# A fused attention and mixture-of-experts kernel: order of the last expert tiles, blocks of the ending, a sum on VectorE, and the check on the softmax sums

## The chip, the cores and the metric

The kernel runs on one core of a Trainium2 chip. The metric is the device time of one launch in microseconds (us), taken as the median of the runs. Beside it there is one profiled execution, from which every duration below comes.

## The reference

The input is one image `x` of 256 channels and 48 x 48 positions, all in float32. The 2304 positions are called tokens. Two layers follow each other.

```python
# layer 0: group norm, then softmax attention over all 4 x 2304 = 9216 head rows
x = x + conv_attention(group_norm(x), Wq, Wk, Wv, Wo)
# layer 1, on tokens t[2304, 256]: attention through 64 slices, then a mixture of 8 experts
t = t + slice_attention(layer_norm(t), W0, Ws, Wqkv, Wout)
xf = layer_norm(t)
top_w, top_i = top_k(xf @ Wg + bg, 2)            # two experts for each token
w = one_hot(top_i) * softmax(top_w)
for e in range(8):
    t = t + w[:, e] * (gelu(xf @ W1[e] + b1[e]) @ W2[e] + b2[e])   # 256 -> 1024 -> 256
out = t transposed back to channels x positions
```

## The kernel before

**Layer 0.** The queries are walked in `NQB` = 18 blocks of 512. For each block the loop runs over 36 pairs of key tiles. TensorE makes scores `s`, ScalarE makes `p` = exp(`s`), VectorE adds `p` into `acc`, and TensorE multiplies `p` with the values into `av`. No row maximum is subtracted. So the kernel keeps, for each block, the largest partial sum and the smallest sum: `extremes()` writes both into `ends_of`, reading `both` in SBUF and the sums `pb` in PSUM. `invert()` has by then written `rinv` = 1/`pb`. Small pieces of work such as these are popped from a list, one after each pair. Much later `judge()` reduces `ends_of`, compares it with `HIGH` and `LOW`, and leaves a flag `bad`. All engines read this flag at the very end, and a branch on it skips a second, safer computation.

**Routing.** VectorE finds the two best experts of each token: `first_max` writes a 0/1 mask into `sel[:, 0]` and then `sel[:, 1]`, each 128 partitions x 18 token tiles x 8 experts. TensorE counts them over the partitions into `pto` (with a matrix of ones) and `pin` (with a triangle, `not_before`). A scan over `pto` on VectorE gives `upto`, and from there a chain on VectorE, ScalarE (`what`) and TensorE (`pw`) gives the list `slot_t`, which says what token lies in which row of which expert tile. The matmuls into `spin`, issued by `busy(n, bank)`, compute nothing that is used.

**Experts.** There are `SURE` = 36 tiles of 128 rows that are always there, numbered 0 to 35, after a few extra ones. For a tile s, the pieces are:

- `rows` gathers its tokens (GpSimd, an indirect DMA) and `load_w1` its weights (SyncE), two tiles ahead;
- `turn` transposes the rows on TensorE (`pt`), and VectorE copies them to `xT`;
- `first` multiplies with W1 in 32 TensorE instructions into `ph`, and ScalarE makes 8 Gelus into `hid`;
- `second` multiplies with W2 in 16 TensorE instructions into `py`, and VectorE adds the bias and scales with the routing weight into `y`;
- `scatter` adds `y` into the token array `t_d` in HBM (GpSimd, an indirect DMA that reads and writes). One scatter waits for the one before to have landed.

TensorE's order is written out by hand: first(s), then second(s-1) with turn(s+1) inside it. At the end of the loop this gives, in short, F33 S32 F34 S33 S34 F35, and then the ending.

**Ending.** The last tile, 35, is not scattered. SyncE loads `t_d` back in the five blocks of `TBLOCKS`, from the last (256 tokens) to the first (512 each), once scatter 34 has landed. Meanwhile TensorE runs S35. Then, for each block and each half `c` of the channels, `columns` transposes the loaded tokens into a bank of `ph` (three banks in turn), a matmul with `here` (which row of tile 35 belongs to which token) adds the contribution of tile 35, and VectorE (`c` = 0) or ScalarE (`c` = 1) copies the bank to `ob`. The write to the output is issued by SyncE, for the last two blocks by ScalarE. TensorE runs one `columns` ahead of the matmul with `here`.

Nearly all instructions bear line 58 in the profile, since a helper issues them. They are told apart by their tiles.

Of the kernel before, what the change touches and what calls it, by code (L numbers as in the profile page):

```python
# [9 lines left out]
FP = mybir.dt.float32  # L10
AF = mybir.ActivationFunctionType
ALU = mybir.AluOpType
AX = mybir.AxisListType
PSUM = bass.MemoryType.PSUM

P = 128
C = 256
NT = 2304
NTT = NT // P
# [7 lines left out]
LOW, HIGH = 1e-12, 1e20  # L27
# [3 lines left out]
E = 8  # L31
# [6 lines left out]
SURE = 2 * NT // P  # L38
FAR = SURE + 3


TBLOCKS = [(t, min(512, NT - t)) for t in range(0, NT, 512)]


def bc(ap, shape):
# [18 lines left out]
def layers(  # L64
# [14 lines left out]
    pe, dve, act, pool = (InOrder(tc, e) for e in (nc.tensor, nc.vector, nc.scalar, nc.gpsimd))  # L79
# [3 lines left out]
    ones = const.tile([P, P], FP, name="ones")  # L83
# [5 lines left out]
        out=gmat, in_=gmat, pattern=[[-8, 16], [0, 8]], compare_op=ALU.is_ge,  # L89
# [3 lines left out]
        out=gmat, in_=gmat, pattern=[[8, 16], [0, 8]], compare_op=ALU.is_ge,  # L93
# [11 lines left out]
    not_before = const.tile([P, P], FP, name="not_before")  # L105
    nc.gpsimd.memset(not_before, -1.0)
    nc.gpsimd.affine_select(
        out=not_before, in_=not_before, pattern=[[-1, P]], compare_op=ALU.is_ge,
# [96 lines left out]
    for h in range(H1):  # L205
        at = ((h // 2) % 2 * 2 + h // 4) * D1
        nc.sync.dma_start(
            out=Wout_sb[at : at + D1, h % 2, 0:C], in_=Wout[h * D1 : (h + 1) * D1, :]
# [25 lines left out]
    with proj, tc.tile_pool(name="ps_pj", bufs=5, space=PSUM) as ps_pj, tc.tile_pool(  # L234
        name="ps_spun", bufs=1, space=PSUM
    ) as ps_spun, tc.tile_pool(
        name="ps_w", bufs=2, space=PSUM
# [41 lines left out]
        pb = ps_w.tile([P, 512], FP, name="pw", tag="pw")  # L279
# [6 lines left out]

        for bi, (t0, tn) in enumerate(TBLOCKS):
            toks = slice(t0, t0 + tn)
# [36 lines left out]
        for i in range(NTT):  # L325
            pv = ps_pj.tile([P, 512], FP, name="pp", tag="pp")
            for c in range(2):
                nc.tensor.matmul(
                    pv[:, 0:C], xn[:, c, i * P : (i + 1) * P], WvT[:, c, :],
                    start=(c == 0), stop=(c == 1),  # L330
# [11 lines left out]
        for ci in range(2):  # L342
            cols = slice(ci * P, (ci + 1) * P)
            for k in range(2):
                nc.tensor.matmul(
                    pw[:, ci * S : (ci + 1) * S], W0T[:, k, cols], Ws_sb[:, k, :],
                    start=(k == 0), stop=(k == 1),
                )
            for k in range(2):
                nc.tensor.matmul(  # L350
                    pw[:, 192 + ci * E : 192 + (ci + 1) * E], WoutT[:, k, cols], Wg_sb[:, k, :],
                    start=(k == 0), stop=(k == 1),
# [20 lines left out]
    ends_of = const.tile([P, 2, NQB], FP, name="ends_of")  # L373

    def busy(n, bank):

        for _ in range(n):
            pe.matmul(bank[:, 0:256], ident, Wqkv_sb[:, 0, 0:256], start=True, stop=True)
# [9 lines left out]
    def in_turn(work):  # L388

        return [w for _, w in sorted(work, key=lambda rank_work: rank_work[0])]  # L390
# [105 lines left out]
    def attention():  # L496


        with tc.tile_pool(name="pexp", bufs=5) as pexp, tc.tile_pool(
            name="att", bufs=2  # L500
        ) as at_p, tc.tile_pool(name="ps_s", bufs=2, space=PSUM) as ps_s, tc.tile_pool(
            name="ps_av", bufs=1, space=PSUM
# [104 lines left out]
            def between(b, st):  # L607

                work, pa, pb = follow(b if b < NQB - 1 else NQB + 3)

                for j in range(2):
                    pe.matmul(
                        pb[j * DK : (j + 1) * DK, 256:512], ones[:, 0:DK],
                        st["both"][:, j * TG : (j + 1) * TG], start=True, stop=True,
                    )

                if b == NQB - 1:
                    busy(7, pa)
                rinv = at_p.tile([P, TG], FP, name="rinv", tag="rinv")

                def invert():
                    dve.reciprocal(rinv, pb[:, 256:512])

                def divide():
                    dve.tensor_mul(OT[:, (b // 2) % 2, b % 2, :], st["o"], rinv)

                def extremes():
                    dve.tensor_reduce(ends_of[:, 0, b : b + 1], st["both"], AX.X, ALU.max)
                    dve.tensor_reduce(ends_of[:, 1, b : b + 1], pb[:, 256:512], AX.X, ALU.min)

                work.extend([(0, invert), (1, divide), (11, extremes)])
                return in_turn(work)
# [4 lines left out]
            for b in range(NQB):  # L637
                row = largest(b) if shifted else None
                st = {}
                for pair in range(NPAIR):  # L640
                    p = scores(b, pair, row)
# [71 lines left out]
    for c in range(2):  # L713
        for i in range(NTT - 2, NTT):
# [3 lines left out]
                start=(i == NTT - 2), stop=(i == NTT - 1),  # L718
# [16 lines left out]
    gp = gating.enter_context(tc.tile_pool(name="gate", bufs=1))  # L735
# [3 lines left out]
    with tc.tile_pool(name="sa", bufs=1) as sa, sums_done, tc.tile_pool(  # L739
        name="ps_sc", bufs=1, space=PSUM  # L740
# [9 lines left out]
        with tc.tile_pool(name="ps_b", bufs=3, space=PSUM) as ps_b:  # L750
# [6 lines left out]
            for m in range(2):  # L757
                for c in range(2):
                    pe.matmul(
                        ph[:, m, :], W0_sb[:, c, m * P : (m + 1) * P], ts_sum[:, c * S : (c + 2) * S],  # L760
                        start=(c == 0), stop=(c == 1),
# [28 lines left out]
            for u in range(2):  # L790
                ph = ps_b.tile([P, 2, 2 * S], FP, name="ph", tag="mm")
                phs.append(ph)
                for kind in range(2):
                    j = 2 * kind + u
                    for c in range(2):
# [3 lines left out]
                            start=(c == 0), stop=(c == 1),  # L799
# [66 lines left out]
            for w in range(2):  # L866
                pe.matmul(
                    pw, tokT[:, w].rearrange("p a s -> p (a s)"), Wout_sb[:, w, :],
                    start=(w == 0), stop=(w == 1),
# [19 lines left out]
        with tc.tile_pool(name="ps_y0", bufs=1, space=PSUM) as ps_y0:  # L889
# [3 lines left out]
            for g, (i0, n) in enumerate(groups):  # L893
                pys = [next(banks)[:, 0 : C + E] for _ in range(n)]
                for i in range(i0, i0 + n, 4):
                    some = range(i, min(i + 4, i0 + n))
                    for k in some:
# [4 lines left out]
                            stop=(k < 4 or k in by_dve),  # L902
# [4 lines left out]
                for k, py in enumerate(pys):  # L907
                    i = i0 + k
# [15 lines left out]
                    out=t_d[i0 * P : (i0 + n) * P, :].rearrange("(i p) c -> p i c", p=P),  # L924
# [13 lines left out]
    with gating, tc.tile_pool(name="onehot", bufs=1) as oh, tc.tile_pool(  # L938
        name="ps_lg", bufs=1, space=PSUM
# [11 lines left out]
        sel = gp.tile([P, 2, NTT, E], FP, name="sel")  # L951
# [18 lines left out]

        pto = ps_lg.tile([P, E * NTT], FP, name="pto")
        pin = ps_lg.tile([P, E, NTT], FP, name="pin")
        for k in range(2):
            for out, m in ((pto.rearrange("p (e i) -> p e i", e=E), ones), (pin, not_before)):
                pe.matmul(
                    out, m, sel[:, k].rearrange("p i e -> p e i"), start=(k == 0), stop=(k == 1)
                )

        e2 = gp.tile([P, NTT], FP, name="e2")
        dve.tensor_sub(e2, m2, m1)
# [72 lines left out]
        k = 0  # L1055
        for n in (3, 6, 6, 3, 6, 6, 3, 3):
# [13 lines left out]
            for j in range(k, k + n):  # L1070
# [3 lines left out]
                    start=(j == 0), stop=(j == K - 1),  # L1074
# [20 lines left out]
    with tc.tile_pool(name="ps_h", bufs=1, space=PSUM) as ps_h, tc.tile_pool(  # L1095
        name="ps_y", bufs=1, space=PSUM
    ) as ps_y, tc.tile_pool(name="ps_t", bufs=1, space=PSUM) as ps_t, tc.tile_pool(
        name="ps_j", bufs=1, space=PSUM
# [8 lines left out]
        ring_ph, ring_py = ring(ps_h, 3, [P, 4, P], "ph"), ring(ps_y, 2, [P, C], "py")  # L1107
# [64 lines left out]
        def second(s, hid, meanwhile):  # L1172

            e = expert_of(s, mybir.EngineType.PE)
            py = next(ring_py)
            for f in range(NHC):
                pe.matmul(
                    py, hid[:, f, :],
                    w2_sb[:, bass.ds(e, 1), f, :].rearrange("p e d -> p (e d)"),
                    start=(f == 0), stop=(f == NHC - 1),  # L1180
                )
                if f == 2:
                    meanwhile()
            e = expert_of(s, mybir.EngineType.DVE)
            y = next(ring_y)
            dve.tensor_tensor(
                y, py, b2_e[:, bass.ds(e, 1), :].rearrange("p e d -> p (e d)"), ALU.add
            )
            dve.tensor_scalar(y, y, slot_w[:, s : s + 1], None, ALU.mult)
            return y  # L1190

        def scatter(s, y):

            indirect(
                out=t_d[:, :], out_offset=bass.IndirectOffsetOnAxis(ap=slot_t[:, s : s + 1], axis=0),
                in_=y, in_offset=None, bounds_check=NT + P - 1, oob_is_err=True,
                compute_op=ALU.add,
            )

        near = range(SURE, FAR)  # L1200
        xs, w1, xT, hid = {}, {}, {}, {}
# [18 lines left out]
        def turn_next(s):  # L1220
            if s in xs:
                xT[s] = turn(xs.pop(s))

        def judge():

            both = fp.tile([P, 2], FP, name="both", tag="judge")
            for k, op in enumerate((ALU.max, ALU.min)):
                dve.tensor_reduce(both[:, k : k + 1], ends_of[:, k, :], AX.X, op)
            dve.tensor_scalar(both[:, 0:1], both[:, 0:1], HIGH, None, ALU.is_gt)
            dve.tensor_scalar(both[:, 1:2], both[:, 1:2], LOW, None, ALU.is_lt)  # L1230
            dve.tensor_tensor(both[:, 0:1], both[:, 0:1], both[:, 1:2], ALU.max)
            pm = ps_j.tile([1, P], FP, name="pm")
            pe.transpose(pm, both[:, 0:1], ident)
            dve.tensor_reduce(bad, pm, AX.X, ALU.max)
# [18 lines left out]
        for s in range(SURE):  # L1253
            hid[s] = first(s, xT.pop(s), w1.pop(s))
            if s + 2 < SURE:
                xs[s + 2], w1[s + 2] = rows(s + 2, next(ring_xs)), load_w1(s + 2, next(ring_w1))
            if s == 0:
                turn_next(1)
            elif s < SURE - 1:
                scatter(s - 1, second(s - 1, hid.pop(s - 1), lambda: turn_next(s + 1)))  # L1260
            if s == SURE - 2:

                scatter(s, second(s, hid.pop(s), lambda: None))
            if s == 4 and bad is not None:
                judge()
            if s == 6:
                pool.iota(
                    here, pattern=[[1, NT]], base=0, channel_multiplier=0,
                    allow_small_or_imprecise_dtypes=True,
                )  # L1270
                dve.tensor_copy(held, slot_t[:, SURE - 1 : SURE])
            if 8 <= s < 8 + len(TBLOCKS):
                t0, n = TBLOCKS[s - 8]
                dve.tensor_scalar(here[:, t0 : t0 + n], here[:, t0 : t0 + n], held, None, ALU.is_equal)

        sp = InOrder(tc, nc.sync)
        blocks = []
        for t0, n in TBLOCKS[::-1]:
            tt = t_flat[:, t0 // P * C : (t0 + n) // P * C].rearrange("p (k c) -> p k c", c=C)

            sp.dma_start(out=tt, in_=t_d[t0 : t0 + n, :].rearrange("(p k) c -> p k c", p=P))
            blocks.append((t0, n, tt))
        y = second(SURE - 1, hid.pop(SURE - 1), lambda: None)
        pts = {}

        def columns(b, c):
# [11 lines left out]
        for at, (b, c) in enumerate(todo):  # L1298
            if at + 1 < len(todo):
                columns(*todo[at + 1])  # L1300
            t0, n, _ = blocks[b]
# [68 lines left out]
```

## Time and profile before

| what | us |
|---|---|
| median of 3 runs (lowest to highest) | 1610.36 (1609.46 to 1611.43) |
| the profiled execution: its own time | 1610.54 |
| the profiled execution: span, first to last instruction | 1608.50 |
| TensorE busy in the span | 1582.4 (98%) |
| VectorE, ScalarE, GpSimd busy | 1043.5, 822.3, 138.1 |
| attention of layer 0 ends at about | 1239 |
| first expert tile starts on TensorE | 1303.5 |
| S35 ends on TensorE | 1586.4 |

Busy time says which engine is loaded over the whole. For the ends of a stage, read the chain of waits (what ended last, followed back) and the timeline (start, duration, instruction, and in brackets how long the engine had been idle and what ended that). TensorE's clock can be granted in full or in part, which the table of windows lists as PEclk.

### The profile page before, as it was taken

Reading aid. Unit: us, or ns where it says so; the run is one execution under the profiler, and the core shown is the slowest. Engines: PE = TensorE matmul, PEld = TensorE weight load, DVE = VectorE, ACT = ScalarE, POOL = GpSimd, SP = SyncE. Lnnn points to the kernel's source line nnn. Section 1 sums busy time; section 2 is a strip of 40 time slices with the busy share of each in tenths; the row PEclk is TensorE's granted clock in tenths of the full one; section 3 lists DMA queues with packets and bytes.
Section 4 is the critical chain, followed back from the end, with each engine's and each line's share of the span. In section 5 each row is a group of like instructions: output and inputs, shape, how many; then the busy total and the mean of one; then the engine's idle time right before and its main releaser. Section 6 shows DMA issues by size and latency. Waiting matters only on the chain. (4 is left out here: it accounts for less than half of the span.)

```text
span 1608.5 us, 32017 instructions
## 1 busy us (share of the span) xinstructions
PE 1582.4 (98%) x13287; PEld 795.0 (49%) x13287; DVE 1043.5 (65%) x1378; ACT 822.3 (51%) x1143; POOL 138.1 (9%) x124
## 2 busy tenths in 40 slices
PE   7999999999999999999999999999999999999997
PEld 3633343333333333333333333333334789999996
DVE  6577777777786877878878778787787731111111
ACT  2355565655655656556556555565654433323331
POOL 0000000000000000000000000000000123433331
PEclk9999999999999999999999999999999999999999
DMA  4000000000000000000000000000000956666664
GB/s 138 0 1 1 1 1 1 1 1 1 1 1 1 2 1 1 1 1 2 1 1 1 1 1 1 1 1 1 1 2 21 331 161 185 175 191 174 187 182 145
DMA packets 37783, 77.58 MB, mean 48 GB/s; under 512 B 3533, under 2 KB 23834, under 8 KB 37498
## 3 DMA queue, kind: packets, MB, share of 16 engines
q1 hardware_dynamic: 29738, 64.25, 11.8%
q0 software_dynamic: 7344, 10.10, 3.7%
q8 instruction: 109, 1.79, 0.5%
q10 hardware_dynamic: 544, 1.05, 0.2%
q14 instruction: 48, 0.39, 0.1%
HBM read 63.07 MB, written 12.32 MB: 47 GB/s over the span
## 5 line engine op out<-in xcount | busy, mean ns | idle before, releaser
L58 ACT ACTIVATE p<-s 128x1024 f32<-128x1024 f32 x648 | 663.5, 1024 | 489.5 <-PE s L58 479.4
L58 DVE TENSOR_TENSOR acc<-acc,p 128x1024 f32<-128x1024 f32 x612 | 748.0, 1222 | 251.6 <-ACT p L58 243.5
L58 PE MATMUL av<-p,v_sb 64*64 64x512 f32 x5184 | 675.7, 590 | 1.0 <-DVE up L58 0.7
L58 PE MATMUL s<-q,kk 64*64 64x512 f32 x5184 | 676.6, 591 | 0.0
L58 PEld LDWEIGHTS s<-q,kk 64*64 64x64 f32 x5184 | 202.2, 133 | 352.0 <-issue 181.3
L58 PEld LDWEIGHTS av<-p,v_sb 64*64 64x64 f32 x5184 | 195.9, 131 | 358.1 <-ACT p L58 202.7
L58 ACT ACTIVATE hid<-ph,bcol 128x128 f32<-128x128 f32 x312 | 89.4, 368 | 199.3 <-PE ph L58 198.6
L58 PE MATMUL py<-w_sb,hid 128*128 x624 | 146.9, 379 | 0.0
L58 PEld LDWEIGHTS ph<-xT,w 128*128 128x128 f32 x1248 | 145.3, 192 | 2.7 <-issue 0.8
L58 PE MATMUL ph<-xT,w 128*128 128x128 f32 x1248 | 145.7, 275 | 0.6 <-issue 0.6
L58 POOL TENSOR_TENSOR rstd_t<-ve,mhalf 128x1 f32<-128x1 f32 (+3 forms) x22 | 28.2, 1280 | 1230.3 <-DVE ve L58 1230.3
L58 DVE COPY xT<-pt 128x256 f32<-128x256 f32 x39 | 16.6, 425 | 160.6 <-PE pt L58 160.6
L58 PEld LDWEIGHTS py<-w_sb,hid 128*128 128x128 f32 x624 | 112.8, 190 | 12.3
L1121 POOL DMA_INDIRECT t_d<-y,slot_t x38 | 60.0, 1578 | 163.7 <-DVE y L58 145.9
L58 DVE TENSOR_TENSOR y<-py,b_bc 128x256 f32<-128x256 f32 x39 | 16.6, 425 | 77.3 <-PE py L58 77.3
L1121 POOL DMA_INDIRECT xs<-tn_d,slot_t x36 | 39.1, 1087 | 15.5 <-issue 10.1
L58 DVE RECIPROCAL rinv<-pb 128x256 f32<-128x256 f32 x18 | 31.5, 1749 | 0.0
L58 DVE TENSOR_TENSOR acc<-p 128x1024 f32<-128x1024 f32 x18 | 22.1, 1226 | 9.9 <-ACT p L58 9.9
L316 DVE TENSOR_SCALAR q<-pp,bcol 64x512 f32<-64x512 f32 (+1 forms) x30 | 20.8, 694 | 7.4 <-PE pp L299 7.1
L58 DVE TENSOR_REDUCE up<-av 128x512 f32<-128x1024 f32 x18 | 21.9, 1216 | 0.0
L58 PE MATMUL spin<-Wqkv_sb,ident 128*128 128x256 f32 x90 | 20.9, 381 | 0.0
L58 PEld LDWEIGHTS spin<-Wqkv_sb,ident 128*128 128x128 f32 x90 | 16.7, 190 | 2.2
(286 smaller groups left out, 627.6 us busy)
## 6 DMA issues: line engine op xcount, KB each, us to landing
w<-in_L_ffn_W_dram SPq DMA_DIRECT2D x39, 1024.0 KB, 5.9
w_sb<-in_L_ffn_W_dram SPq DMA_DIRECT2D x8, 1024.0 KB, 13.0
t_sb<-t_d SPq DMA_DIRECT2D x4, 512.0 KB, 7.1
x_sb<-in_x_dram SPq DMA_DIRECT2D x3, 576.0 KB
t_d<-t_sb SPq DMA_DIRECT2D x2, 768.0 KB, 6.5
tn_d<-tn SPq DMA_DIRECT2D x2, 768.0 KB
b_bc<-in_L_ffn_b_dram SPq DMA_DIRECT2D x1, 1024.0 KB
out_dram<-ob SPq DMA_DIRECT2D x2, 512.0 KB
```

The lines of the kernel that those rows point to most:

```text
L58: return self.tc.keep_in_program_order(getattr(self.engine, name)(*args, **kwargs))
L316: nc.vector.tensor_scalar(dst, pq[rows, 0:tn], bcol[rows, B_Q + m : B_Q + m + 1], 0.125, ALU.add, ALU.mult,)
L1121: new = nc.gpsimd.indirect_dma_start(**kwargs)
```

## The change

Five edits, all in one step.

1. The last three scattered tiles follow each other differently. TensorE's order becomes F33 S32 S33 F34 S34 F35, then the ending. The turn of tile 35 moves from S33 into S34.
2. The ending has six blocks, in a list of its own: first the block of 256 tokens as before, then three of 512, then two of 256. The last two are issued by ScalarE, as before.
3. Three matmuls of 128 x 256, that compute nothing used, stand on TensorE between S35 and the first `columns`.
4. VectorE adds the two masks of `sel` into `both`, in the order experts by tiles, and TensorE counts this sum with two matmuls in place of four.
5. `extremes` takes the largest of `rinv` in place of the smallest of `pb`, and `judge` reduces both halves of `ends_of` in one instruction.

```diff
+ENDBLOCKS = [(2048, 256), (0, 512), (512, 512), (1024, 512), (1536, 256), (1792, 256)]
...
-                    dve.tensor_reduce(ends_of[:, 1, b : b + 1], pb[:, 256:512], AX.X, ALU.min)
+                    dve.tensor_reduce(ends_of[:, 1, b : b + 1], rinv, AX.X, ALU.max)
...
+        both = gp.tile([P, E, NTT], FP, name="both")
+        dve.tensor_tensor(both.rearrange("p e i -> p i e"), sel[:, 0], sel[:, 1], ALU.add)
+        bothf = both.rearrange("p e i -> p (e i)")
         pto = ps_lg.tile([P, E * NTT], FP, name="pto")
+        pe.matmul(pto, ones, bothf, start=True, stop=True)
         pin = ps_lg.tile([P, E, NTT], FP, name="pin")
-        for k in range(2):
-            for out, m in ((pto.rearrange("p (e i) -> p e i", e=E), ones), (pin, not_before)):
-                pe.matmul(
-                    out, m, sel[:, k].rearrange("p i e -> p e i"), start=(k == 0), stop=(k == 1)
-                )
+        pe.matmul(pin.rearrange("p e i -> p (e i)"), not_before, bothf, start=True, stop=True)
...
-            for k, op in enumerate((ALU.max, ALU.min)):
-                dve.tensor_reduce(both[:, k : k + 1], ends_of[:, k, :], AX.X, op)
+            dve.tensor_reduce(both, ends_of, AX.X, ALU.max)
             dve.tensor_scalar(both[:, 0:1], both[:, 0:1], HIGH, None, ALU.is_gt)
-            dve.tensor_scalar(both[:, 1:2], both[:, 1:2], LOW, None, ALU.is_lt)
+            dve.tensor_scalar(both[:, 1:2], both[:, 1:2], 1.0 / LOW, None, ALU.is_gt)
...
-            elif s < SURE - 1:
+            elif s < SURE - 2:
                 scatter(s - 1, second(s - 1, hid.pop(s - 1), lambda: turn_next(s + 1)))
-            if s == SURE - 2:
-                scatter(s, second(s, hid.pop(s), lambda: None))
+            if SURE - 3 <= s < SURE - 1:
+                scatter(s, second(s, hid.pop(s), lambda: turn_next(s + 1) if s == SURE - 2 else None))
...
-        for t0, n in TBLOCKS[::-1]:
+        for t0, n in ENDBLOCKS:
...
         y = second(SURE - 1, hid.pop(SURE - 1), lambda: None)
+        busy(3, next(ring_py))
```

The instructions of the built program differ in these places only. On SyncE, six loads stand where five did, and four output writes where three did. GpSimd's list is the same.

## Prediction

> **What bounds the kernel now.** The page gives TensorE 98% of the span, but four of the five edits lie in two places where TensorE waits or runs dummies, so I read those places: the chain of waits near the end, the timeline there, the table of windows for the clock, and the timeline of the routing.
>
> The chain of waits from 1577 us (start, length, what):
>
> ```profile
> 1577.08 3.75 DMA t_d<-y,slot_t
> ...
> 1581.58 3.87 DMA t_d<-y,slot_t
> ...
> 1585.91 3.73 DMA t_sb<-t_d
> 1589.64 0.04 issue
> 1589.68 12.72 PE ph L58 x50
> 1602.40 0.02 issue
> 1602.43 0.59 ACT ob L58
> ```
>
> Two scatters run one behind the other, then the reload of `t_d`, then TensorE without a gap until the last copy. From that copy's start to the span's end are 6.07 us. The timeline says why scatter 34 starts at 1581.58:
>
> ```profile
> 1579.91 0.35 DVE L58 TENSOR_SCALAR y<-y,slot_w 128x256 f32<-128x256 f32 x1
> 1581.30 1.14 ACT L58 ACTIVATE hid<-ph,bcol 128x128 f32<-128x128 f32 x4 [7.77 <-PE ph L58]
> 1581.58 1.55 POOL L1121 DMA_INDIRECT t_d<-y,slot_t  x1 [2.94 <-DMA t_d<-y,slot_t]
> 1582.71 3.33 PEld L58 LDWEIGHTS py<-w_sb,hid 128*128 128x128 f32 x16
> 1582.82 3.62 PE L58 MATMUL py<-w_sb,hid 128*128 x16
> 1583.08 1.14 ACT L58 ACTIVATE hid<-ph,bcol 128x128 f32<-128x128 f32 x4 [0.64 <-PE ph L58]
> ```
>
> Its `y` was done at 1580.26; the release is scatter 33. Note also S35 (1582.82), which follows F35 at once and doesn't stall although half its Gelus come at 1583.08.
>
> The windows of the ending (TensorE busy comes first, PEclk before the DMA share):
>
> ```profile
> 1586.50:1589.90 3.40, 1.31 (x8) 0.91 (x9) 1.17 (x3) 0.00 (x0) 0.00 (x0) 1.00 0.93 322
> 1589.90:1593.30 3.40, 3.40 (x12) 2.44 (x11) 0.00 (x0) 0.37 (x1) 0.00 (x0) 0.51 0.99 373
> 1593.30:1596.70 3.40, 3.40 (x18) 2.06 (x17) 0.94 (x2) 0.59 (x1) 0.00 (x0) 0.99 0.23 86
> ```
>
> After S35 TensorE is busy 1.31 of 3.40 us; in the next 3.40 us it has half its clock.
>
> The timeline of the routing, around the count of the choices:
>
> ```profile
> 1279.71 0.68 PE L58 MATMUL pto<-sel,ones 128*128 128x144 f32 x2
> 1280.22 0.70 PE L58 MATMUL pin<-sel,not_before 128*128 128x144 f32 x2
> 1280.74 0.70 PE L58 MATMUL pto<-sel,ones 128*128 128x144 f32 x2
> 1281.26 0.70 PE L58 MATMUL pin<-sel,not_before 128*128 128x144 f32 x2
> 1281.48 0.45 DVE L58 TENSOR_TENSOR_SCAN upto<-same_e,pto 128x144 f32<-128x144 f32 x1 [1.41 <-PE pto L58]
> ```
>
> The second mask is ready at 1279.98, yet the scan starts at 1281.48: VectorE waits 1.41 us for four matmuls that follow each other by 0.52 us.
>
> [...] a pass over 144 masks, read with a step of 8 floats, takes 0.26 us, while a dummy pass over 256 contiguous columns takes 0.22 (2.56 us for 11). [...] ScalarE's last branch is at 1603.8, its next event at 1607.2. [...] Here 512 elements from SBUF take 679 ns and 256 from PSUM 414.
>
> **The change part by part.**
>
> *Choices (edit 4).* Added: one sum of 144 elements on VectorE, 0.31 us as the neighbouring 128x144 rows. It starts when `sel` can be read, 0.34 after 1279.67 by the pitch of its neighbours, so 1280.01 to 1280.32. The output is strided, which no row shows for this operation; bounds 0.25 to 0.65, the fastest and slowest mask rows, and I take 0.31. Then `pto`: 144 contiguous columns are 144/256 of 0.22 a pass, 0.25 for two, plus 0.17 from the last pass to its recorded end and 0.1 for the wait, so the scan starts at about 1280.86. Gain 0.62 (0.3 to 0.7). Behind the sum on VectorE waits `e2`, later by 0.34, with ScalarE's exponent, table load and six rows of `tn` behind it, which end at 1285.35 instead of 1285.01. ScalarE's first `what` is thus bound by `tn` and gains little; but by the second group VectorE is what ScalarE waits for (idle 0.86 us ahead of 1288.54), so the chain keeps its 0.62 down to `slot_t`, the gathers and the first tile. The dummies between are fixed in number, so they move along.
>
> *Extremes and judge (edit 5).* 18 reductions of 256 elements read SBUF instead of PSUM. The 679 ns row less 256 elements at about 1.04 ns is again 0.41: nothing. Cover: in the attention (140 to 1240 us) TensorE is busy 1097 of 1100, VectorE 857, so 0.38 us are free for each of 648 pairs. `judge` issues one small reduction less while `pm` waits on TensorE: 0.05 (0 to 0.1).
>
> *Order of the tiles (edit 1).* TensorE's work is only permuted. S33 can follow S32, since its Gelus end at 1566.3 and S32 at 1568.55. S34 directly behind F34 is as S35 behind F35: no stall. F34's rows are turned in S32 as before; tile 35's are turned in S34, 2 us ahead of F35; both W1 loads landed long before. So S34 still ends at 1579.25 and `y` at 1580.26. S33 now ends near 1572.0; scatter 33 waits for scatter 32 (landed 1573.64), goes at about 1574.4 as scatter 34 did 0.74 after its release, and lands at 1578.3. GpSimd has nothing else to issue behind it. Scatter 34 then waits for `y` only: 1580.26 + 0.28 (as scatter 32 after its `y`) = 1580.54 instead of 1581.58. The reloads move by **1.04** (0.6, if the slower release of 0.74 stays, to 1.1).
>
> *Dummies and blocks (edits 2, 3).* S35 still ends at 1586.4; the dummies, 6 passes of 0.22, hold TensorE until 1587.6. The first reload (TensorE on it at 1588.18) lands by 1587.1 and the second (1589.64) at 1588.6, so TensorE goes on without a gap and keeps its clock. Warm prices, from the pitch of 1.30 for each half block of 512 in 1593.6 to 1600: 0.44 for four transposes, 0.86 for the product with `here`; half of each for 256. That brings TensorE to the transposes of the third block at 1590.8. The trace gives that load 6.3 us from issue at 1586.38, so 1592.7; earlier by 1.04 it is **1591.65**, and TensorE waits 0.9 us. From there the rest: transposes 2.6, products 6.0, sum 8.6; and in the blocks of 256 a bank of `ph` is wanted 0.64 us after its product was streamed while the copy behind a 512 block needs 0.17 + 0.59 + 0.2, so about 0.4 of waiting on copies. TensorE's record ends at 1591.65 + 8.6 + 0.4 + 0.17 = 1600.82, against 1602.39: 1.57. The last copy on ScalarE takes 0.37 instead of 0.59: 0.22. Added on SyncE: one load issue (0.34) behind the fourth, in nobody's way, and one output write more, of block 3, ahead of what ScalarE issues. The last write is half as large, but that gives nothing: [...]
>
> *Sum.* 0.62 + 0.05 + 1.57 + 0.22 = 2.46. Against the profiled time, 1610.54 (span 1608.50 and 2.04 around it): 1608.1. That execution lies 0.18 over the median, so 1607.9 for the median.
>
> **The rivals.**
>
> A, the above: 1607.9. *Chance 0.48.*
>
> B, the third load doesn't bind. Second and third landed 3.05 us apart, the third and fourth 1.3; the first gap may be a hiccup. Then TensorE goes on at 1590.8 and 0.88 more is won: 1607.0. Against it: the DMA share is 0.93 to 0.99 then. *0.25.*
>
> C, the clock still closes. In A TensorE idles 0.9 us of a window (74% busy), and in the routing some 0.5 + 0.75 us around shorter matmuls. The trace has 82% in 1284 to 1288 at full clock and 39% that lost it; nothing between. A closed window costs 1.7 us: 1609.6. *0.16.*
>
> D, the change doesn't do what it says at the end: scatter 34 is released no earlier and TensorE's dummies only take the place of idle time; the routing's part is left, and the copy: 1609.5. *0.05.*
>
> E, slower: VectorE's reduction of `rinv`. If the SBUF source doubled it to 0.83 and none of it were covered, 18 x 0.41 = 7.4 less 2.5 would give 1615.2. It decides from 0.14 us exposed in each block. Against it: the 679 ns row, and 0.38 us free per pair. *0.06.*
>
> **How the numbers follow.** About 0.2% (3.2 us) is what a measurement of this kernel can tell from no change. Around each case lie some 0.6 us for the bounds above and the spread of runs. Faster by over 3.2, under 1607.1: 0.6 of B and a quarter to a third of A, near 0.30. Slower by over 3.2: E, 0.06. The rest, 0.64, is within. The range 1605.9 to 1609.9 takes in A, B with its spread, and C and D up to theirs.
>
> **What would show it.** Right: scatter 34 starts about 0.3 us after its `y`; PEclk stays at 1.00 after S35; TensorE waits for a `t_sb` load once, before the third block; the scan starts within 1 us of the second mask; the ending from S35 to the last copy's start shrinks from 16.0 to about 14.4 us. Wrong: a stall between F34 and S34, a PEclk of 0.5 anywhere after 1280 us, or `ends_of<-rinv` above 0.5 us.

## The result, and the profile after

The changed kernel takes 1607.59 us, median of 20 runs (1605.85 to 1608.61). The kernel before, run beside it, takes 1610.05 (1608.23 to 1612.13, 20 runs). The ratio is 0.9985, with a 95% interval of 0.9979 to 0.9991. So it is faster, by 2.46 us in the medians, and by less than the 3.2 us that were named as the bound of what can be told from no change. The prediction had 1607.9 as its likeliest time. The profiled execution of the changed kernel took 1607.27 us, its span 1605.0. One run of old_order, an experiment below, took 2001.07 us at a granted clock of 0.786, and is left out of that experiment's numbers.

The chain of waits of the changed kernel, from scatter 34 on:

```profile
1578.80 3.72 DMA t_d<-y,slot_t
...
1583.47 6.20 DMA t_sb<-t_d
1589.66 0.14 issue
1589.80 6.47 PE ph L60 x28
...
1596.98 1.97 PE ph L60 x10
1598.95 0.02 issue
1598.97 0.37 ACT ob L60
```

There is one scatter where two stood. The reload on the chain is now the third, issued at 1583.47 and landed at 1589.66. In the timeline of the changed kernel the same place reads:

```profile
1578.17 0.35 DVE L60 TENSOR_SCALAR y<-y,slot_w 128x256 f32<-128x256 f32 x1
1578.80 1.55 POOL L1123 DMA_INDIRECT t_d<-y,slot_t  x1 [4.35 <-DVE y L60]
1581.08 3.62 PE L60 MATMUL py<-w_sb,hid 128*128 x16
1584.54 1.46 PE L60 MATMUL py<-Wqkv_sb,ident 128*128 128x256 f32 x6
1589.80 0.63 PE L60 MATMUL ph<-ident,t_sb 128*128 128x128 f32 x4 [0.47 <-DMA t_sb<-t_d]
```

Scatter 34 starts 0.28 us behind its `y` (1578.52), released by `y` itself. The dummies follow S35. TensorE waits 0.47 us for a reload ahead of the third block. The windows of the changed kernel (TensorE busy first, then four engines, PEclk, DMA share):

```profile
1583.10:1586.50 3.40, 3.40 (x20) 2.98 (x18) 0.78 (x2) 0.00 (x0) 0.00 (x0) 1.00 0.82 272
1586.50:1589.90 3.40, 2.87 (x15) 1.51 (x14) 0.90 (x2) 0.37 (x1) 0.00 (x0) 1.00 0.96 341
1589.90:1593.30 3.40, 3.40 (x18) 2.10 (x18) 0.83 (x2) 0.59 (x1) 0.00 (x0) 1.00 0.59 211
```

The clock stays at 1.00 up to the last product. (It falls to half at 1602.80, behind 3.41 us in which TensorE had no work, and in the kernel before at 1607.04, behind as many.) The routing, in the timeline of the changed kernel:

```profile
1278.25 0.40 DVE L60 TENSOR_TENSOR both<-sel 128x144 f32<-128x144 f32 x1
...
1278.80 0.48 PE L60 MATMUL pto<-both,ones 128*128 128x144 f32 x2 [0.69 <-DVE e L60]
...
1279.32 0.45 DVE L60 TENSOR_TENSOR_SCAN upto<-same_e,pto 128x144 f32<-128x144 f32 x1 [0.65 <-PE pto L60]
```

VectorE still waits ahead of the scan, but 0.65 us instead of 1.41.

The two profiles differ by 3.48 us of span, more than the medians. To see where, I cut every profile at the same marks: the start of the last `rinv`, the first matmul of the next stage (`pm`), the start of the second mask, the scan, the first tile's first matmul (F), the end of S35, the start of the last copy on ScalarE, and the end. "Branch" is the recorded time of TensorE's taken branch ahead of the first tile. The column "clock" says whether PEclk fell to half between S35 and TensorE's last product. All in us, from one profiled execution each; the experiments are told below.

| kernel | start to `rinv` | `rinv` to `pm` | mask to scan | scan to F | branch | F to S35 end | S35 end to last copy | clock | copy to end |
|---|---|---|---|---|---|---|---|---|---|
| before | 1236.12 | 3.98 | 1.81 | 21.98 | 3.43 | 282.98 | 15.99 | half | 6.07 |
| before_again | 1235.29 | 3.98 | 1.79 | 22.39 | 3.83 | 282.97 | 14.28 | open | 6.27 |
| before_c | 1236.49 | 3.98 | 1.80 | 22.45 | 3.93 | 282.98 | 14.61 | open | 6.07 |
| only_check | 1236.27 | 2.93 | 1.80 | 22.04 | 3.47 | 282.98 | 14.93 | open | 6.18 |
| check_last_only | 1235.51 | 2.93 | 1.80 | 21.86 | 3.35 | 283.00 | 14.11 | open | 6.16 |
| only_choices | 1235.66 | 3.98 | 1.41 | 22.41 | 3.89 | 283.26 | 16.03 | half | 6.55 |
| choices_b | 1236.10 | 3.98 | 1.41 | 22.04 | 3.53 | 283.72 | 15.90 | half | 6.12 |
| only_ending | 1236.51 | 3.98 | 1.80 | 21.93 | 3.37 | 282.98 | 14.37 | open | 5.85 |
| after | 1235.38 | 2.93 | 1.41 | 22.40 | 3.85 | 282.98 | 14.27 | open | 6.05 |
| after_again | 1235.80 | 2.93 | 1.41 | 21.87 | 3.37 | 282.98 | 13.69 | open | 5.99 |
| no_dummies | 1236.04 | 2.93 | 1.41 | 22.45 | 3.94 | 283.77 | 14.45 | open | 6.01 |
| old_blocks | 1236.10 | 2.93 | 1.41 | 22.61 | 4.10 | 283.25 | 13.59 | open | 6.83 |
| old_order | 1235.59 | 2.93 | 1.41 | 22.61 | 4.09 | 286.07 | 14.61 | open | 6.04 |
| five_banks | 1235.86 | 2.93 | 1.41 | 22.12 | 3.53 | 283.85 | 16.27 | open | 5.59 |

So the pair of profiles, before less after, reads: 0.74 in the start (where no edit lies), 1.05 between `rinv` and `pm`, 0.40 at the scan, 0.42 given back between the scan and F, 1.72 in the ending, and some hundredths. The span from `pm` to the mask is 39.6 us in every profile. F to S35's end is 282.98 in the pair. In six of the experiments it is longer, by 0.3 to 3.1 us; all six have edit 4, and they are taken up with it below.

### The profile page after: what moved, and what is told of

Same layout as the page of the kernel before. It is cut to its first block, busy times and chain, and to the rows that moved or that the text cites. A ratio compares the mean times of both kernels' runs of the same rounds, so it can differ in the third digit from the quotient of the medians.

```text
span 1605.0 us, 32039 instructions
## 1 busy us (share of the span) xinstructions
PE 1580.8 (98%) x13293; PEld 793.3 (49%) x13293; DVE 1043.7 (65%) x1379; ACT 822.4 (51%) x1144; POOL 138.0 (9%) x124
## 3 DMA queue, kind: packets, MB, share of 16 engines
q8 instruction: 109, 1.79, 0.5%
## 5 line engine op out<-in xcount | busy, mean ns | idle before, releaser
L60 DVE TENSOR_TENSOR acc<-p 128x1024 f32<-128x1024 f32 x18 | 22.1, 1225 | 9.9 <-ACT p L60 9.9
L60 DVE TENSOR_REDUCE up<-av 128x512 f32<-128x1024 f32 x18 | 21.9, 1216 | 0.0
```

What stands on the lines that cost most here:

```text
L60: return self.tc.keep_in_program_order(getattr(self.engine, name)(*args, **kwargs))
```

## The experiments

**Once more the kernel before.** There is no edit.

> The kernel before, profiled once more, to see how far its intervals repeat. If they are properties of the program: last reciprocal to the first matmul of the next stage 3.99 us, second mask to the scan 1.81, first tile's first matmul to the end of S35 282.98, end of S35 to the last copy on ScalarE 15.99, TensorE's taken branch ahead of the first tile 3.43. If the branch is noise, as one theory has it, it differs from 3.43 by some 0.4 here already; if the change lengthened it, it stays at 3.4.

Measured: ratio 0.9997 (0.9988 to 1.0005), as it should be. The marks up to the scan repeat within 0.02 us, apart from the start. The ending doesn't: 14.28 us in place of 15.99. Its windows, same program, cut as those of before were:

```profile
1586.50:1589.90 3.40, 1.77 (x11) 1.37 (x12) 0.78 (x2) 0.00 (x0) 0.00 (x0) 1.00 1.01 353
1589.90:1593.30 3.40, 3.40 (x19) 2.24 (x19) 0.69 (x1) 0.73 (x2) 0.00 (x0) 1.00 0.94 355
```

PEclk is 1.00 where the first profile had 0.51. So the ending of the kernel before has two lengths, and the prediction was worked out on the long one. TensorE's branch is 3.83 here: its length is no mark of the change.

**The check alone (edit 5).**

```diff
-  dve.tensor_reduce(ends_of[:, 1, b : b + 1], pb[:, 256:512], AX.X, ALU.min)
+  dve.tensor_reduce(ends_of[:, 1, b : b + 1], rinv, AX.X, ALU.max)      # and judge() as in the change
```

> The kernel before with edit 5 alone (the check from the reciprocals). Theory 'bank': the last of the 18 reductions holds a PSUM bank that the next stage writes first; the wait of 1.11 us on ends_of goes, last reciprocal to first matmul falls from 3.99 to 2.93 us, and the time falls by 1.0 us (ratio 0.9994). Rival, the prediction's own step: the edit is worth nothing, the interval stays near 4.0 and the 1.06 seen in the pair of profiles came from elsewhere; ratio 1.0000.

Measured: 1608.97 us against 1610.20, ratio 0.9993 (0.9985 to 1.0001). `rinv` to `pm` is 2.93 us. First the line of the kernel before, from its timeline:

```profile
1240.11 0.41 PE L58 MATMUL pm<-ident,x_sb 128*128 128x128 f32 x2 [1.11 <-DVE ends_of L58]
```

Then the timeline of this kernel:

```profile
1239.20 0.44 PE L58 MATMUL pm<-ident,x_sb 128*128 128x128 f32 x2
1239.47 1.03 PE L58 MATMUL pm<-WoT,OT 128*128 128x256 f32 x4
1239.69 0.41 DVE L58 TENSOR_REDUCE ends_of<-rinv 128x1 f32<-128x256 f32 x1
```

In the first, TensorE had been idle for 1.11 us until VectorE's reduction of `pb`. In the second, the matmul runs half a microsecond ahead of the reduction, which takes the same 0.41 us. The 2.93 us are what theory "bank" had for the stretch from `rinv` to `pm`. The 95% interval of the time reaches just past 1; its middle, 1.1 us, agrees with the 1.05 us that the traces show. The clock in the ending, told below, could have helped by chance: of the kernel before, 18 of the 49 runs beside it are listed with a mean clock of 0.997, of this one none of 13. Among the runs with 0.998 alone the difference is 1.0 us (1609.98 in 8 runs, 1609.02 in 9).

**The check in the last block alone.** The check on the sums is not the same here: for the last block it looks at the smallest reciprocal.

```diff
-  dve.tensor_reduce(ends_of[:, 1, b : b + 1], pb[:, 256:512], AX.X, ALU.min)
+  last = rinv if b == NQB - 1 else pb[:, 256:512]
+  dve.tensor_reduce(ends_of[:, 1, b : b + 1], last, AX.X, ALU.min)
```

> The kernel before, whose last block alone reduces rinv where the first 17 reduce the sums in PSUM. The check on the sums is no longer the same: for the last block it looks at the smallest reciprocal. Theory 'bank': only the last reduction counts, since only behind it a new stage takes the bank; last reciprocal to first matmul 2.93 us, as with all 18. Rival: the reductions inside the attention hold up TensorE too, and the span from the first to the last reciprocal is shorter with all 18 changed than here by more than 0.2 us.

Measured: 2.93 us again, 1607.23 us in its one run. From the first to the last reciprocal there are 1095.9 us with none, one and all 18 changed. So 17 of the 18 reductions cost nothing, and the last one cost 1.05 us. The run takes away the one read and the wait goes with it. That the wait is for the PSUM bank of `pb`, which the next stage's pool takes over, fits the code and both runs; no run shows directly that the pools are laid out so.

**The choices alone (edit 4).**

```diff
-  for k in range(2): (pto with ones, pin with not_before) <- sel[:, k], read across
+  dve.tensor_tensor(both.rearrange("p e i -> p i e"), sel[:, 0], sel[:, 1], ALU.add)
+  pe.matmul(pto, ones, bothf, ...); pe.matmul(pin, not_before, bothf, ...)
```

> The kernel before with edit 4 alone (the sum of the two masks on VectorE). Both theories expect the second mask to the scan at 1.41 us instead of 1.81. Theory 'carried': scan to the first tile's first matmul stays near 22.0 and the time falls by 0.4 us. Theory 'absorbed': that interval grows by what was won, to 22.4, because TensorE's taken branch takes 3.85 instead of 3.43; the time doesn't fall.

> Edit 4 alone once more, for the length of TensorE's taken branch ahead of the first tile. So far: without edit 4, 3.43, 3.83, 3.47 and 3.37 us; with it, 3.89, 3.85, 3.37, 3.94, 4.10 and 4.09. Theory 'the edit lengthens it': 3.8 or more again. Theory 'noise': either. The scan starts 1.41 us behind the second mask.

Measured: ratio 1.0001 (0.9993 to 1.0009) for the first; 1610.98 us in the one run of the second. The scan comes 0.39 us earlier behind the mask in both, as in every kernel with the edit. The branch was 3.89 and then 3.53 us. Over all profiles it is 3.35 to 3.93 without the edit and 3.37 to 4.10 with it, so "the edit lengthens it" falls as a rule. What stands between the scan and F follows the branch: 21.9 to 22.1 where it is 3.4 to 3.5, and 22.4 to 22.6 where it is longer. A gain of 0.4 us is smaller than the 0.75 us by which this branch varies.

There is a second loss, behind F. F to S35's end is 282.97 to 283.00 us in all six profiles without edit 4, and 282.98 in two of the eight with it; in the other six it is longer by 0.27 to 0.87, and in old_order by 3.09. Apart from a clock in old_order that is told there, the first delay in these six comes at the same place, a tile's first matmul with W1 some 33 us behind F; in three of them the profile names the load of `w`. The row of choices_b, from its timeline:

```profile
1336.42 3.81 PE L58 MATMUL ph<-xT,w 128*128 128x128 f32 x32 [0.30 <-DMA w<-in_L_ffn_W_dram]
```

Why the load is late there is not known, and that edit 4 makes it late is a pattern of fourteen profiles, not a shown cause. But from the second mask to S35's end the kernels with the edit are on average no faster than those without. So no run shows that the 0.4 us reaches the time; the interval holds both 0.4 us less and nothing.

**The ending alone (edits 1, 2 and 3).** The diff is that of the change, in these three places.

> The kernel before with edits 1, 2 and 3 (order of the last tiles, blocks, dummies). The prediction has 1.79 us for these: end of S35 to the last copy on ScalarE 14.3 us instead of 16.0, PEclk at 1.00 there, span's end 6.0 us behind that copy; ratio 0.9989. The other intervals as before: 3.99 and 1.81. A rival that puts part of the whole gain into the start of the program would show the ending at under 1.2 us of gain.

Measured: 1608.64 us against 1610.20, ratio 0.9991 (0.9984 to 0.9997). The ending is 14.37 us with the clock open, as expected, the other intervals as before. But the profile of the kernel before with which it was to be compared is one of two. Of seven profiles with the old ending three have half a clock (15.90 to 16.03 us) and four an open one (14.11 to 14.93). Their mean is 15.1; the three with edits 1 to 3 as in the change have 13.69 to 14.37, mean 14.1. So, on the means of these few profiles, the three edits are worth about 1.9 us where the clock would have closed and some 0.4 where not.

**Once more the changed kernel.** There is no edit.

> The changed kernel, profiled once more. In the kernel before, end of S35 to the last copy on ScalarE was 15.99 us in one profile, with TensorE's clock at half for 3.4 us, and 14.28 in another of the same program, with the clock open. Theory 'clock phase': the ending of before has two lengths, by where the clock's window falls, and the changed one has one; so 14.3 again here, PEclk 1.00. Rival: the changed ending also varies by over a microsecond. TensorE's taken branch ahead of the first tile: 3.4 or 3.85, as in the two profiles of before, if it is noise; 3.85 if the change did it.

Measured: 1607.36 us, ratio 0.9983 (0.9977 to 0.9990). The clock is open, the branch 3.37 us. The ending is 13.69, and TensorE doesn't wait for the third reload here. So cases A and B of the prediction are both true, each of some executions.

**Without the dummies (edit 3 undone).**

```diff
-  busy(3, next(ring_py))
```

> The changed kernel without edit 3 (the three dummies between S35 and the first transposes). The prediction let the third reload bind, so without the dummies TensorE begins some 0.7 us earlier on the first block and waits that much longer for the third load: 14.3 us from S35's end to the last copy if the clock stays open, and the dummies are worth nothing. Theory 'clock phase': TensorE then idles some 0.6 plus 1.7 us, so the clock closes in some executions: about 1.7 us more in those, ratio to before higher by up to 0.0005 in the median.

Measured: 1607.10 us, ratio 0.9985 (0.9978 to 0.9992), the same as the whole change. From this kernel's timeline:

```profile
1591.47 0.63 PE L60 MATMUL ph<-ident,t_sb 128*128 128x128 f32 x4 [0.98 <-DMA t_sb<-t_d]
```

TensorE waits 0.98 us for the third reload where it waited 0.47 with the dummies, and the ending is 14.45 us: what was won ahead is waited for there. The clock stayed open in this one profile, and wherever a window of 3.41 us (the step that is told with before_c) is laid in its ending, TensorE is busy for at least 2.38 us of it. The dummies thus show no worth once the reloads come earlier. Three of the 17 runs are listed with a clock of 0.997, as none of the changed kernel is, and take 1.8 us longer than the others (1608.94 against 1607.15); where they lost it no profile shows.

**With the old blocks (edit 2 undone).**

```diff
-  for t0, n in ENDBLOCKS:
+  for t0, n in TBLOCKS[::-1]:
```

> The changed kernel without edit 2 (the ending in the five old blocks). By the prediction's sum the two short blocks cost about 0.4 us of waiting for banks and save 0.22 us in the last copy, and the smaller last write is worth nothing: end of S35 to the last copy's start 13.9 us, the span's end 6.3 behind it, so about 0.2 us faster than the changed kernel. Rival: the last write sets the end, which then comes some 0.6 us later than that: 6.9 us behind the copy's start, 0.4 us slower than the changed kernel.

Measured: 1607.81 us, ratio 0.9988 (0.9981 to 0.9994). The ending is 13.59 us to the last copy, and 6.83 from there, where the changed kernel has 6.05. That is the rival's number, but not its mechanism. On the line of the last branch this kernel has:

```profile
L1335 SPq EVENT_SEMAPHORE  x9: 17/17/17, 1599.4 to 1603.7; - x9
L1335 ACTq EVENT_SEMAPHORE  x2: 17/17/17, 1604.4 to 1604.5; - x2
L1335 ACTq COMPARE_BRANCH  x1: 59/59/59, 1600.9 to 1600.9; - x1
```

and the changed kernel:

```profile
L1335 SPq EVENT_SEMAPHORE  x9: 17/17/17, 1601.1 to 1603.3; - x9
L1335 ACTq EVENT_SEMAPHORE  x2: 17/17/17, 1603.2 to 1603.2; - x2
L1335 DVEq EVENT_SEMAPHORE  x2: 21/21/21, 1603.3 to 1603.4; - x2
L1335 ACTq COMPARE_BRANCH  x1: 59/59/59, 1600.2 to 1600.2; - x1
```

ScalarE, not the write that SyncE waits for, is last with the old blocks: from its branch to its next event are 3.5 us, against 3.0 with a last write half as large. In all eight profiles with a last write of 512 KB it is 3.4 to 3.9; in the six with 256 KB, 2.9 to 3.0. So the blocks count by way of the wait behind ScalarE's branch. That it is the size of the last write is likely, but not shown: with the new blocks the branches of the engines also lie differently to each other, and TensorE's own takes 4.3 to 4.6 us instead of 3.4 to 4.0.

**With the old order (edit 1 undone).**

```diff
-  F33 S32 S33 F34 S34 F35
+  F33 S32 F34 S33 S34 F35
```

> The changed kernel without edit 1 (order F33 S32 F34 S33 S34 F35). Scatter 34 waits for scatter 33 again and starts 4.85 us ahead of S35's end instead of 5.90; the reloads start 1.05 later. If the third reload binds, as the prediction has it, end of S35 to the last copy grows by the same, to about 15.3 us, and the time by 1.0 us. If TensorE's work binds, it grows by 0.3 at most.

Measured: 1608.17 us, ratio 0.9988 (0.9980 to 0.9996). Scatter 34 starts 4.89 us ahead of S35's end and the reloads 1.03 later than with the new order, as expected. The ending is 14.61 us, not 15.3: 0.9 longer than in after_again, where TensorE didn't wait for the third reload either, and 0.3 longer than in the first profile of the change, where it did. TensorE waits 0.31 and 0.55 us for the first two reloads here. So the reloads bind in both orders, but with the old one not the third; in time the difference lies within the intervals.

This profile took 1611.04 us, for another reason: F to S35's end is 286.07. In its windows, cut at the marks that are told with before_c, the clock is at half for 3.42 us at the first tile:

```profile
1299.20:1302.61 3.41, 1.61 (x10) 1.01 (x9) 0.42 (x1) 0.00 (x0) 2.49 (x4) 1.00 0.33 101
1302.61:1306.03 3.42, 3.42 (x18) 3.42 (x18) 0.00 (x0) 0.49 (x2) 0.89 (x1) 0.50 0.26 79
```

The window with 1.61 us takes in the end of TensorE's branch of 4.09 us. The first tile takes 1.63 us longer for it.

**Five banks at the end.**

```diff
-  pts[b, c] = next(ring_ph)...
+  pts[b, c] = next(ring_pt if n == 256 and b > 0 else ring_ph)...
```

> The changed kernel, with the transposes of the two last blocks in the two banks of pt (idle by then) in place of the three banks of ph. The prediction charged some 0.4 us to waiting for copies there; the changed profile shows TensorE idle 0.53 and 0.47 us ahead of weight loads released by copies to ob. If that is on the path, end of S35 to the last copy is shorter by 0.4 to 0.8 us for the same landing of the third reload (13.4 with no wait for it, 13.9 with), and the time by as much, which a ratio can hardly show. If the copies themselves pace the end, nothing is won.

Measured: 1607.96 us, ratio 0.9987 (0.9980 to 0.9993), no better than the change. The ending is 16.27 us. The design was at fault: the four half blocks use the two banks of `pt` in turn, which is one fewer than before, and the timeline shows TensorE idle for 0.52 and 0.51 us until copies to `ob` from these banks; it also waited 1.30 for the third reload. It says nothing on a ring of five.

**The kernel before a third time.** There is no edit.

> The kernel before a third time, for the same branch and for the clock in the ending. Theory 'the edit lengthens it': 3.4 to 3.5; theory 'noise': either. End of S35 to the last copy: near 16.0 with PEclk at half for 3.4 us, or 14.3 to 14.9 with it open; nothing between, if the clock's window is the cause.

Measured: 1610.26 us in its one run; the branch 3.93 us, the ending 14.61 with an open clock. Both are as "noise" and the clock's window had it.

The trace records when the granted clock changes. In the profile of before it falls to half at 67.63, 1589.97 and 1607.04 us: 446 and 5 times 3.413 us apart. In old_order it falls at 66.99, 1302.61 and 1606.40: 362 and 89 times 3.413. In the first profile of the change it falls at 66.81 and 1602.80, 450 times 3.413 apart. So in these three profiles all falls of one execution lie on marks 3.413 us apart, and the marks lie differently to the program in each. Laid out from there, these are the window behind S35 in which TensorE waits most, and the one after it, of before:

```profile
1586.56:1589.97 3.41, 1.38 (x9) 0.98 (x10) 1.11 (x3) 0.00 (x0) 0.00 (x0) 1.00 0.95 329
1589.97:1593.38 3.41, 3.41 (x12) 2.37 (x11) 0.00 (x0) 0.37 (x1) 0.00 (x0) 0.50 0.98 369
```

and of before_c:

```profile
1587.69:1591.10 3.41, 1.66 (x11) 1.26 (x12) 0.83 (x3) 0.00 (x0) 0.00 (x0) 1.00 0.98 359
1591.10:1594.51 3.41, 3.31 (x17) 1.88 (x17) 0.69 (x1) 0.37 (x1) 0.00 (x0) 1.00 0.98 343
```

From 1240 us on, every window with TensorE busy for 1.61 us or less of 3.41 is followed by half a clock in the 14 profiles (1.21, 1.38 and 1.58 in the three endings, 1.61 in old_order, and those behind the last product), and none with 1.66 or more is. (That isn't all there is to it: the fall at 67.63 comes behind a window in which TensorE is busy for all 3.42 us.) So in the endings at hand the two lengths go with how much of TensorE's waiting lies between two marks: 1.38 us busy in before, 1.66 in before_c.

The mean clock of each single run agrees. In the profiles it is 0.997 in the four with a half clock in the ending or at the first tile, and 0.998 or 0.999 in the other ten. Of the 137 runs of the kernel before beside the experiments, 46 have 0.997 or less, and they take 1.6 us more than the rest (means of 1611.18 and 1609.57). Of the 41 runs of the changed kernel none has it.

## Why the prediction was right

The time was right, and so was the direction. That the sum of 2.46 us is also the difference of the medians is luck: one step was much too small, two were too large, and they cancel.

- *Order of the tiles.* Right. Scatter 34 was released by its `y` after 0.28 us, as said; no stall between F34 and S34; the reloads are issued 1.1 us earlier against S35's end (1.9 to 2.2 ahead of it, instead of 0.9 to 1.1), where 1.04 was forecast.
- *Ending, 1.57 + 0.22.* Right for the profile that it was worked out on: 15.99 became 14.27, forecast 14.4. From TensorE's start on the third block to the end of the last product 9.13 us passed, forecast 9.17. TensorE's wait for that block was 0.47 us in one profile and none in the next, forecast 0.9. The 0.22 of the shorter last copy doesn't show: from the copy to the end there are 6.05 us, and were 6.07. The failed step is the one that let one profile stand for the kernel before. Its half clock came in three of seven profiles with the old ending, and in a third of its runs, so in the mean of the profiles the ending gained about 1.0 us.
- *"The last write is half as large, but that gives nothing".* Wrong: with the new blocks there are 2.9 to 3.0 us from ScalarE's last branch to its next event, and 3.4 to 3.9 with the old ones. What ScalarE waits for there no run shows. In the pair the shorter wait doesn't show, since with the new blocks the events of SyncE, ScalarE and VectorE on that line end within 0.2 us of each other (1603.3, 1603.2 and 1603.4).
- *Choices, 0.62.* The sum of the masks, with its strided output, took 0.40 us in place of 0.31, and TensorE started 0.15 behind it, so 0.40 was won at the scan. That the chain "keeps its 0.62" down to the first tile was not shown: TensorE's branch varies by more, and behind F most profiles with the edit lose as much again. The mark "within 1 us of the second mask" was missed, with 1.10.
- *Extremes and judge, 0.05.* The step that failed. The duration was right (0.409 us from SBUF, 0.414 from PSUM), and that 17 of 18 are covered too. What was missed is who waits for the last one: 1.05 us of TensorE's time. The profile of before had the row, a wait of `pm` for `ends_of`, and the prediction priced the operation without asking for its waiters.
- *Case C* (the clock still closes) did not occur in the ending of any profile with edits 1 to 3. Its other place did: in old_order, which has edit 4, the clock fell to 0.50 at the first tile. In the first profile of the change the window there had TensorE busy for 1.81 us. The prediction knew windows of 82% and 39% and "nothing between"; from 1240 us on the 14 profiles have half a clock behind windows of up to 1.61 us of 3.41 and a full one behind 1.66 and more (47 and 49%). *Case E* (slower, by the reduction of `rinv`) is excluded: that reduction takes 0.41 us.

Measured one by one, the parts give 1.1 (check), no gain that shows (choices) and 1.4 us (ending), against 2.4 to 2.7 for the whole.

## What to carry to other kernels

Price an instruction that is moved from PSUM to SBUF by who waits for it, above all at the end of a stage, where the next one's first matmul may stand behind it; its own duration may not change at all (0.41 us here from both). Before a stall in one profile is put into a sum, see whether it is in the next profile of the same program: here half a clock came in the ending of three of seven profiles with the old ending, and 46 of 137 runs of the kernel before have the lower mean clock that goes with it. And of a gain of some tenths of a microsecond, ask what random wait stands between it and the end.

## What the runs showed of the hardware that was not expected

- Half a clock in the same program comes and goes. In the profiles of before, the change and old_order its starts lie on marks 3.413 us apart, and the marks lie differently to the program in each. TensorE need not be idle for it: from 1240 us on, with 1.61 us busy between two marks or less the next 3.41 us ran at half the clock in the 14 profiles, with 1.66 or more they did not. Runs of the kernel before with a mean clock of 0.997 or less take 1.6 us more than the others.
- A taken branch on TensorE took 3.35 to 4.10 us at the same place of the program, with no cause found. VectorE's branch on the same line was over in 0.07 us, and its next event came 0.2 us after (1298.4 to 1298.6 in the first profile), so VectorE did not wait there as TensorE did.
- The third of the reloads lands late in some executions (wait of 0.47 to 1.30 us on TensorE) and on time in others.
- From ScalarE's last branch to its next event there are 2.9 to 3.0 us in the six profiles with a last write of 256 KB and 3.4 to 3.9 in the eight with 512 KB.
